# A planner's account of PSUM reads and engine hops, changed for the second stage of a four-layer graph network

## The chip, the cores and the metric

The kernel runs on one core of one Trainium2 chip. The metric is the device time of one launch in microseconds (us), the median of several runs. TensorE is called PE here, VectorE DVE, ScalarE ACT, GpSimd POOL, and SyncE, which issues most transfers, SP. PEld stands for PE's weight loads.

## What is computed

The input x has 128 graphs of 64 nodes with 256 features, 8,192 rows in all, in float32; adj is one 64x64 matrix. Four layers follow one another, each inside a residual sum and a layer norm. The reference, cut to its core:

```python
x = _layernorm(x + _L0(x))   # three products with adj*adj and W1, W2, W3, relu between them
x = _layernorm(x + _L1(x))   # U.T x, W1, relu, W2, U; U = eigenvectors of the normed Laplacian of adj
x = _layernorm(x + _L2(x))   # two graph convolutions, then four LSTMs over windows of the nodes
x = _layernorm(x + _L3(x))   # attention over the 64 nodes of a graph, masked by adj

# in _L2: window length p = 1..4, one LSTM each; the last state of each window replaces its last node
for p in range(1, MAX_SKIP + 1):
    nw = Tv // p
    wins = h[:, :nw * p, :].reshape(Bv * nw, p, Hd)
    last = _lstm_last(Wih[p - 1], Whh[p - 1], bih[p - 1], bhh[p - 1], wins)
    h = h.at[:, jnp.arange(nw) * p + (p - 1), :].set(last.reshape(Bv, nw, Hd))
# one LSTM step
g = x_t @ Wih.T + h @ Whh.T + bias
i, f, gg, o = jnp.split(g, 4, axis=-1)
c = sigmoid(f) * c + sigmoid(i) * tanh(gg)
h = sigmoid(o) * tanh(c)
```

## The kernel before

The rows are cut into 64 tiles of 128 rows, and four tiles make a group, so there are 16 groups. The program has two stages.

**First stage.** It does layer 0 for all groups, and the eigenvectors of one 64x64 matrix beside it, as a long chain of small DVE operations. Its products are recorded at line 926 and those of the eigenvectors at line 286. The change doesn't touch this stage.

**Second stage.** It does layers 1, 2 and 3 group by group. No order of instructions is written in the code. The functions `layer1`, `layer2`, `layer3`, `lstm` and `second` only note operations with the class `Plan`; `Plan.run` then keeps up to four groups (WAYS = 4) under way at once and puts the noted operations into an order. It is a list scheduler: for each engine it looks for the operation that could start earliest by its own account of time, takes the earliest one over all engines, emits it to that engine's queue, and moves the account on. [...] Every instruction emitted so has line 154 in the profile, the line in `emit`.

The account works with three kinds of numbers. A cost is how long an operation holds its engine: for DVE 0.067 + n/960 us for n elements in a partition, for ACT 0.158 + 0.00084 n where it reads PSUM, for PE 0.001673 n + 0.003 us for each product (at least 0.223). LAG (line 110) is the stated hop: how long after that cost another engine may use the result. OWN (line 113) is the same for the engine itself. All are in us.

What waits for what is found in `note` (lines 123 to 147). Each operation lists the parts of tiles that it writes and reads, and a part is a mask over the elements of the tile. An operation waits in the account for every earlier operation on the same tile whose mask and rows overlap with its own, if one of the two writes. This is the account alone. The waits of the built program are set afterwards, by the layer that records instructions: from the order in which operations were emitted, and with more caution than the account, as the profile will show.

**PSUM in the second stage.** There are eight PSUM banks with the tag "ps", each 512 float32 elements in every partition. Most tiles with this tag are filled by a few products and then read as a whole. Two places read a tile in parts:

- `second` (window length 2, second time step) computes the gates of the LSTM from seven products of sums of quarters in place of eight, for each of two halves h. Its helper `two` puts two of these seven products into one bank, in the first and second half of its columns, and hands back both halves; each half is 2 x 128 columns. Each half takes four products, which show as eight matmul records. Then ACT copies p1, and DVE adds p2, p6, p7, p5, p3 and p4 one after the other.
- `layer3` puts the last products of two row tiles into one bank and adds each of them to X by an operation of its own.

The lines of `second` that matter:

```python
p1, p2 = two(0, 1)
S.copy(u1, p1)
V.tensor_add(a, u1, p2)
p6, p7 = two(5, 6)
V.tensor_add(c12, u1, p6)
V.tensor_add(b, c12, p7)
p5, p3 = two(4, 2)
V.tensor_add(d, b, p5)
V.tensor_add(c12, c12, p5)
V.tensor_add(c12, c12, p3)
p4, _ = two(3)
```

In the profile the products with sums of quarters are `ps<-w,sums` and `ps<-hs,sums`, and the DVE additions are `gates<-v,ps` (p2, p6) and `gates<-gates,ps` (p7, p5, p3, p4).

Of the kernel before, what the change touches and what calls it, by code (L numbers as in the profile page):

```python
# [103 lines left out]
class Plan:  # L104
# [2 lines left out]

    LAG = {"PE": 0.205, "DVE": 0.16, "ACT": 0.15, "POOL": 0.0, "SP": 2.0}  # L110

    MOST = {"w": 3, "v": 2, "ps": 4, "gates": 2}
    OWN = {"PE": 0.0, "DVE": 0.125, "ACT": 0.105, "POOL": 0.0, "SP": 0.0}
# [10 lines left out]
    def note(self, engine, calls, cost, ready=0.0):  # L124

        op = Op()
        op.engine, op.calls, op.cost, op.group, op.rank = engine, calls, cost, self.group, len(self.ops)
        op.before, op.after, op.tiles, op.ready, op.start = set(), [], [], ready, None
        for name, args, kw in () if callable(calls) else calls:
            for i, x in enumerate(list(args) + list(kw.values())):  # L130
                if not isinstance(x, Part):
                    continue
                t, write = x.tile, i == 0
                mask = np.zeros(int(np.prod(t.shape[1:])), bool)
                mask[x.at.reshape(-1)] = True
                for other, w, rows, m in t.past:
                    if (w or write) and other is not op and other.start is None and rows[0] < x.rows[1] and x.rows[0] < rows[1] and (m & mask).any():
                        op.before.add(other)
                t.past.append((op, write, x.rows, mask))
                if t not in op.tiles:  # L140
                    op.tiles.append(t)
                    t.left += 1
        op.left = len(op.before)
        for other in op.before:
            other.after.append(op)
        self.ops.append(op)
# [9 lines left out]
    def run(self, groups, ways):  # L156
# [9 lines left out]
        while todo or going:  # L166
# [40 lines left out]
            self.free[e] = t + op.cost  # L207
            end = t + op.cost + self.LAG[e]
            for tile in op.tiles:
# [1329 lines left out]
```

## Time and profile before

| what | value |
|---|---|
| median of three runs | 2520.61 us (2520.24 to 2522.3) |
| the profiled execution's own time | 2522.03 us |
| its span, first to last instruction | 2520.3 us |
| first product of the second stage | at 860.6 us |
| start of the last product | at 2506.2 us |
| PE busy, over the span | 2473.2 us (98%) |
| granted clock of PE | 0.998 |
| HBM traffic | 25.40 MB read, 12.58 MB written |

The span is what the profile's times count from. The profiled execution took 1.7 us more than its span, and it was 1.4 us slower than the median of the runs. Its second stage is some 1,646 us long, with a tail of 14 us of norms and stores after the last product.

A row of the trace's timeline gives the start in us, the duration in us, the engine, the line, the operation, what it writes and reads, and how many were merged into the row; brackets hold the idle time of the engine ahead of it and what ended it. A product of two float32 tiles shows as two matmul records, and matmuls overlap in the record: a matmul with 128 columns is 0.275 us long, and the next one starts 0.112 us after it.

### The profile page before, as it was taken

What the parts mean: (1) busy time and instruction counts of PE and PEld (TensorE: products, weight loads), DVE (VectorE), ACT (ScalarE), POOL (GpSimd) and SP (SyncE); (2) the same over time, 40 slices, a digit from 0 to 9 for tenths busy, and PEclk for the clock granted to TensorE, in tenths of its full rate; (3) what the DMA queues carried; (4) which work ended last, traced back from release to release, by engine and by line L of the source; (5) the groups of instructions that cost most, each with busy time, mean ns of one, the idle gap of its engine ahead of it and who ended that gap; (6) DMA issues with size and microseconds to landing.
All of it is one profiled execution on the core that took longest, in us unless ns stands there. A gap on an engine that the chain in (4) does not pass through costs nothing.

```text
span 2520.3 us, 41153 instructions
## 1 busy us (share of the span) xinstructions
PE 2473.2 (98%) x15788; PEld 2194.3 (87%) x15788; DVE 1523.3 (60%) x5404; ACT 1105.1 (44%) x2754; POOL 139.4 (6%) x317
## 2 busy tenths in 40 slices
PE   9999999999999999999999999999999999999997
PEld 7788888888887889989989899898898998988996
DVE  6888777778885454464554644645546455365336
ACT  2344333333333455444444454444544444445455
POOL 0000000000000100000000000000000001010002
PEclk9999999999999999999999999999999999999999
DMA  4000000000000300000000000000000000000000
GB/s 154 18 10 26 18 17 18 17 18 1 1 1 1 117 1 1 18 18 1 18 18 1 18 1 18 18 1 18 5 5 9 1 9 9 1 9 1 1 1 26
DMA packets 27397, 40.62 MB, mean 16 GB/s; under 512 B 2880, under 2 KB 22080, under 8 KB 27200
## 3 DMA queue, kind: packets, MB, share of 16 engines
q1 hardware_dynamic: 26848, 37.71, 4.4%
q8 instruction: 124, 2.03, 0.3%
q14 instruction: 73, 0.60, 0.1%
q10 hardware_dynamic: 352, 0.28, 0.0%
HBM read 25.40 MB, written 12.58 MB: 15 GB/s over the span
## 4 chain that ended last, share of the span: by engine, by line
PE 91%; DVE 6%; DMA 1%; ACT 1%; issue 1%; POOL 0%; SPq 0%; ACTq 0%; POOLq 0%; DVEq 0%
PE ps L154 60%; PE ps L926 30%; DVE gates L154 2%; ACT gates L154 1%; DVE D L52 1%; DVE X L154 1%; PE pc L286 1%; DMA aw<-in_a_w_dram 0%; DVE c L154 0%; DVE tw L52 0%; POOL rs L154 0%; DVE st L154 0%; DVE w L154 0%; DMA bw<-in_b_w_dram 0%; DMA X<-in_x_dram 0%
## 5 line engine op out<-in xcount | busy, mean ns | idle before, releaser
L154 PE MATMUL ps<-w,wih 128*128 128x128 f32 (+2 forms) x4864 | 839.1, 309 | 1.0 <-ACT v L154 1.0
L154 PEld LDWEIGHTS ps<-w,wih 128*128 128x128 f32 x4864 | 726.6, 191 | 34.7 <-issue 5.0
L154 ACT ACTIVATE gates<-ps,cbi 128x128 f32<-128x128 f32 (+2 forms) x1120 | 447.6, 403 | 508.1 <-PE ps L154 498.2
L154 PE MATMUL ps<-hs,whh 128*128 128x128 f32 (+1 forms) x2816 | 459.3, 286 | 1.7 <-DVE hs L154 1.7
L154 PEld LDWEIGHTS ps<-hs,whh 128*128 128x128 f32 x2816 | 394.9, 191 | 5.4 <-DVE hs L154 3.4
L154 DVE SCALAR_TENSOR_TENSOR gates<-gates 128x256 f32<-128x256 f32 (+2 forms) x256 | 89.9, 351 | 284.2 <-ACT gates L154 283.8
L926 PE MATMUL ps<-aw,h 128*128 128x256 f32 x1024 | 227.2, 379 | 0.0
L926 PEld LDWEIGHTS ps<-aw,h 128*128 128x128 f32 x1024 | 192.9, 190 | 26.0 <-ACT h L935 0.5
L935 ACT ACTIVATE h<-h 128x512 f32<-128x512 f32 x128 | 80.5, 629 | 198.5 <-DVE h L52 198.4
L154 DVE SCALAR_TENSOR_TENSOR c<-gates,c 128x128 f32<-128x128 f32 (+2 forms) x192 | 62.9, 328 | 154.2 <-ACT gates L154 153.2
L154 PE MATMUL ps<-w,sums 128*128 128x128 f32 x896 | 122.5, 280 | 22.7 <-DVE gates L154 22.7
L154 PEld LDWEIGHTS ps<-w,sums 128*128 128x128 f32 x896 | 108.8, 192 | 31.5 <-DVE gates L154 30.7
L154 ACT ACTIVATE gates<-gates,cbi 128x256 f32<-128x256 f32 x128 | 54.9, 497 | 157.8 <-DVE gates L154 157.6
L926 PE MATMUL ps<-ss,tw 128*128 128x256 f32 x512 | 117.9, 380 | 0.0
L926 PE MATMUL ps<-ss,aw 128*128 128x256 f32 x512 | 117.3, 379 | 0.0
L926 PE MATMUL ps<-m,aw 128*128 128x256 f32 x512 | 117.1, 380 | 0.0
L154 DVE SCALAR_TENSOR_TENSOR hs<-gates 128x128 f32<-128x128 f32 (+2 forms) x192 | 62.9, 328 | 87.7 <-ACT gates L154 87.1
L926 PE MATMUL ps<-aw,m 128*128 128x512 f32 x256 | 114.5, 593 | 0.0
L154 POOL TENSOR_SCALAR rs<-mv 128x2 f32<-128x2 f32 x96 | 25.6, 267 | 1530.3 <-DVE mv L154 1529.1
L154 ACT ACTIVATE gates<-c 128x128 f32<-128x128 f32 (+2 forms) x288 | 97.1, 337 | 25.5 <-DVE c L154 24.1
L926 PEld LDWEIGHTS ps<-ss,aw 128*128 128x128 f32 x512 | 96.6, 190 | 12.8
L926 PEld LDWEIGHTS ps<-ss,tw 128*128 128x128 f32 x512 | 96.3, 190 | 12.9 <-issue 0.2
(305 smaller groups left out, 3562.3 us busy)
## 6 DMA issues: line engine op xcount, KB each, us to landing
out_dram<-X SPq DMA_DIRECT2D x64, 128.0 KB, 1.7
X<-in_x_dram SPq DMA_DIRECT2D x30, 256.0 KB, 4.4
rest<-X SPq DMA_DIRECT2D x8, 512.0 KB, 2.6
wih<-in_c_ih_dram SPq DMA_DIRECT2D x4, 1024.0 KB, 7.2
X<-rest SPq DMA_DIRECT2D x8, 512.0 KB, 3.3
aw<-in_a_w_dram SPq DMA_DIRECT2D x3, 1024.0 KB, 10.0
whh<-in_c_hh_dram SPq DMA_DIRECT2D x3, 1024.0 KB, 9.0
aw<-in_a_w_dram SPq DMA_DIRECT2D x1, 512.0 KB, 5.3
```

The costliest lines, as they stand in the source:

```text
L52: return getattr(self.engine, name)(out, *args, **kw)
L154: getattr(e, name)(*[real(x) for x in args], **{k: real(v) for k, v in kw.items()})
L286: PE.matmul(out, lhsT, rhs, start=True, stop=True)
L926: PE.matmul(out, lhsT, rhs, start=start, stop=stop)
L935: S.activation(dst, src, AF.Relu)
```

## The change

There are two edits, both in `Plan`, and both in the account only. The computation stays as it is: the same operations are noted, with the same engines, tiles and costs.

1. A read of a tile with the tag "ps" gets the mask of the whole tile (`...` sets every element). In the account a reader of half a bank so waits for the products of the other half too, where these were noted ahead of it.
2. The stated hop from DVE to other engines goes from 0.16 to 0.13 us and that from ACT from 0.15 to 0.14 us.

```diff
-    LAG = {"PE": 0.205, "DVE": 0.16, "ACT": 0.15, "POOL": 0.0, "SP": 2.0}
+    LAG = {"PE": 0.205, "DVE": 0.13, "ACT": 0.14, "POOL": 0.0, "SP": 2.0}
...
                 t, write = x.tile, i == 0
                 mask = np.zeros(int(np.prod(t.shape[1:])), bool)
-                mask[x.at.reshape(-1)] = True
+
+                mask[... if t.tag == "ps" and not write else x.at.reshape(-1)] = True
                 for other, w, rows, m in t.past:
```

## Prediction

> **What bounds the kernel now.** I began with the page's busy shares, went on to the table by stage, then to who waits for whom on PE, and last to the timeline at one wait. The busy row says that PE is the bound:
>
> ```profile
> PE 2473.2 (98%) x15788; PEld 2194.3 (87%) x15788; DVE 1523.3 (60%) x5404; ACT 1105.1 (44%) x2754; POOL 139.4 (6%) x317
> ```
>
> The change acts only between the first and the last product of the second stage, so that stretch is cut out. The columns are the stretch, its length, and the busy time of PE, PEld, DVE, ACT and POOL.
>
> ```profile
> 860.60:2506.20 1645.60, 1618.22 (x11729) 1495.28 (x11729) 859.99 (x2522) 787.18 (x1975) 97.98 (x201) 1.00 0.03 11
> ```
>
> PE is idle for 1645.60 - 1618.22 = 27.4 us there, while DVE is busy for 860 us and ACT for 787 us, about half of it. Only PE's idle time and the products themselves make this stage long. The waits of PE in this stretch, with total us, times and longest:
>
> ```profile
> PE ps L154 <- DVE gates L154: 22.7, 41, 0.7
> PE ps L154 <- DVE hs L154: 1.7, 2, 0.9
> PE ps L154 <- ACT att L154: 1.0, 2, 0.6
> PE ps L154 <- ACT v L154: 1.0, 2, 0.5
> PE ps L154 <- ACT X L154: 0.6, 1, 0.6
> ```
>
> The five rows make 27.0 of the 27.4 us, and one of them is 22.7: PE fills a bank and waits for DVE, which writes `gates`. The timeline of PE and of DVE at one of the 41:
>
> ```profile
> 1214.14 1.50 PE L154 MATMUL ps<-w,sums 128*128 128x128 f32 x12
> 1216.16 0.94 PE L154 MATMUL ps<-w,sums 128*128 128x128 f32 x6 [0.51 <-DVE gates L154]
> ```
>
> ```profile
> 1214.42 0.42 DVE L154 TENSOR_TENSOR gates<-v,ps 128x256 f32<-128x256 f32 x1 [0.17 <-PE ps L154]
> 1215.68 0.42 DVE L154 TENSOR_TENSOR gates<-v,ps 128x256 f32<-128x256 f32 x1 [0.85 <-PE ps L154]
> ```
>
> DVE's second addition starts at 1215.68, as soon as PE's twelve records are through, and ends at 1216.10; PE goes on at 1216.16. PE waited for a reader which itself had waited for the product right before. The engines take turns where they should overlap. The order of the built program tells why: in the bank of p6 and p7 (and of p5 and p3) the addition of the first half was emitted before the last products of the second half, and the recording layer then makes the next product into that bank wait for the addition, though it writes other columns. The planner didn't know of that wait, since its masks of the two halves don't overlap.
>
> [...] The gap repeats here (three times in the pair step at 1211 to 1226 us, 1.7 us in sum), but what it waits for is a reader of the same tile, so another bank wouldn't end it. [...]
>
> **The change part by part.** The sum is made against the profiled execution, 2522.0 us (span 2520.3 and 1.7 around it). That is 1.4 us above the median of the runs, 2520.6.
>
> *The mask.* It removes no instruction and adds none: 8,120 matmul instructions stand in both built programs. It moves the reads of half banks behind all products of their bank. Comparing the two built orders, before has 69 matmuls in the second stage that wait for an ACT or DVE reader of the bank they write, all in the pair step, and in 41 of these the reader depends on the matmul just before. After has none of the 69. One such wait costs more than its idle time. PE's records start 0.112 us apart and last 0.275, so the idle time in the record begins 0.163 us after the next product was due. Check at the rows above: twelve records from 1214.14 end their turns at 1215.48, the next came at 1216.16, 0.68 us late, which is 0.51 + 0.163. And the six records after it last 0.94 us where 5 x 0.112 + 0.275 = 0.835 would do: 0.10 us more, as the next weight load could not run ahead. Sum: 22.7 + 41 x (0.163 + 0.101) = 33.5 us, all on PE, which sets the end. As a second count, I summed how far each product into `ps` from `sums` starts later than the median spacing of its shape: 34.3 us. The two waits for ACT's `v` (1.0 us) are the same: the copy of p1 ahead of the bank's other half, and with 2 x 0.264 they add 1.5. I take **35.0 us gained**.
>
> *What is late next.* The additions of the first half start up to four products (8 x 0.112 = 0.9 us) later; the copy of p1 is 8 products later in the first pair step (1.8 us). Queued behind them on DVE are the additions of the same bank, then gates of this and other groups; on ACT the gate activations. Who waits for those is PE, at the first product of window length 3, which reads what the pair step wrote. By the orders and spacings, PE has 3.7 to 4.7 us of other products between the two before, and the trace shows no idle time there; after it has 4.2 to 5.2 us in the first 13 groups. The last addition reads p4, whose place hasn't changed. So this costs nothing while that filler stands; without it the chain of one addition (0.42), two activations (0.50 each), two updates of c (0.43 each), a tanh (0.42) and the two writes (0.29 each), some 3.3 us, would show in each of 16 groups. A bank is also held longer by up to 0.9 us; with eight banks the after order has no product which waits for a reader of one of the two matmuls before it, 8 at three matmuls and 16 at four (8 and 11 before), so I price it at nothing.
>
> *The hops.* They change no instruction either, but the order everywhere: PE's, DVE's and ACT's sequences differ in most places, with 1,928 waits of PE for DVE or ACT against 1,841. Is the new hop too short? A DVE operation of 256 elements costs 0.334 us in the account and takes 0.420 in the trace; a matmul released by DVE starts 0.054 us after its end (median of 45). So 0.14 us is the measured hop, and 0.13 is 0.01 us short, where 0.16 was 0.02 us long. For ACT on a bank: 0.373 against 0.471 and 0.053 after the end (7 cases), 0.15 us, so 0.14 is 0.01 us short. Bounds: at most all 1,928 waits come 0.01 us late, 19 us; on the other side the rest of PE's idle time could go, 27.0 - 22.7 - 1.0 = 3.3 us gained. Most waits have slack, as PE idles in 5 other places only; I take 2.0 us lost, some 200 waits of 0.01.
>
> *POOL and SP.* POOL has the same instructions in the same sequence but for the order of groups; SP the same 64 stores of 128 KB and 8 reloads. They follow PE. The DMA queues are 3% busy in this stage. What can move is DVE standing behind POOL's `rs` (X<-rs cost DVE 5.1 us in 9 waits, and two of PE's rows on `hs` stem from such a wait): up to 2 us either way, taken as nothing.
>
> *The tail* after the last product is 14 us of the same norms; the last three products stand in another sequence, by one product of 0.43 us: up to 1 us either way, taken as nothing.
>
> Sum: -35.0 + 2.0 = -33.0 us, so 2489.0 for an execution like the profiled one, and 2520.6 - 33.0 = **2487.6 us** as a median. The case's own range takes 3.3 us gained and 3 more from POOL and the tail below (2481), and hops of 8 us and 3 more above (2497).
>
> **Rivals.** *Part of the stall moves.* The pair step is a dense chain: 56 products of 0.224 us, 12.5 us of PE, and about 20 DVE additions and updates of 0.42 us. The stalls gave DVE time to catch up, and in the account DVE is cheaper than in the trace (0.334 against 0.385 for each of four in a row at 1217.80). If DVE falls behind, each of 16 pair steps gives back about 0.8 us: 13 us, so 2487.6 + 13 = 2501 us. For it: the 10% error. Against: DVE is half idle, and the filler ahead of window length 3 got longer.
>
> *Nothing comes of it.* The waits on half banks could be replaced one for one by waits for whole banks: 2520 us. The 41 to none at one matmul speaks against it.
>
> *Slower.* Reading late holds the banks, and PE waits at the head of the next tile: 16 groups x 2 halves x 4 banks = 128 banks. From 35.0 / 128 = 0.27 us of PE's wait for each bank on, the gain is gone; if the whole 0.45 us, the mean delay of the first half, came through, it would be 58 us, hence 2487.6 + 58 = 2546 us. For it: PE has been without slack. Against: eight banks, and no short loop in the after order.
>
> **How the numbers follow.** Forecast 0.83 (2481 to 2497), stall in part moved 0.10 (2497 to 2506), nothing 0.03, slower 0.04. The range 2481 to 2499 leaves out most of the second case and the last two, with the edges of the first some 0.2. Faster, within and slower than 0.2% (5 us, about what a measurement of this kernel can tell from no change): 0.93, 0.03, 0.04.
>
> **What would show it.** Right: PE's wait for DVE `gates` falls from 22.7 us to under 3; PE's idle time between first and last product from 27 to under 8 us; its busy time there falls also, by some 7 us, since each pause leaves a longer record; `gates<-v,ps` keeps 0.42 us. Wrong: waits of PE on DVE or ACT of many short pieces (hops too short), or a new row of PE waiting at the first product of a bank or of window length 3.

## The result, and the profile after

| | before | after |
|---|---|---|
| median of four runs each | 2520.43 us (2520.13 to 2522.3) | 2485.93 us (2485.29 to 2486.62) |
| the profiled execution's own time, and its span | 2522.03, 2520.3 us | 2486.62, 2484.8 us |
| first product of the second stage | 860.63 us | 859.80 us |
| from there to the start of the last product | 1645.58 us | 1611.15 us |
| from there to the end of the span | 14.1 us | 13.85 us |

The ratio is 0.9862, with a 95% interval of 0.9845 to 0.9879: 34.5 us less by the medians. The spans of the two profiled executions differ by 35.5 us, and 34.4 of these lie between the first and the last product of the second stage, 0.8 ahead of it and 0.25 behind it.

The page of the changed kernel still has PE as the bound:

```profile
PE 2462.3 (99%) x15788; PEld 2191.0 (88%) x15788; DVE 1519.4 (61%) x5404; ACT 1104.5 (44%) x2754; POOL 135.5 (5%) x317
```

The second stage alone, first to last product, with the columns of the prediction's row for this stage (length, then busy time of PE, PEld, DVE, ACT, POOL):

```profile
859.80:2470.95 1611.15, 1607.95 (x11729) 1492.14 (x11728) 856.74 (x2524) 786.60 (x1975) 94.15 (x201) 1.00 0.03 11
```

PE was idle there for 27.4 us and is now for 1611.15 - 1607.95 = 3.2. Who still makes PE wait, in all of the program's products from `emit`:

```profile
PE ps L155 <- ACT X L155: 1.3, 3, 0.9
...
PE ps L155 <- ACT att L155: 0.5, 1, 0.5
PE ps L155 <- ACT v L155: 0.5, 2, 0.3
PE ps L155 <- ACT w L155: 0.4, 2, 0.3
...
PE ps L155 <- DVE hs L155: 0.2, 1, 0.2
```

The row on DVE's `gates`, 22.7 us in 41 waits, is gone. The sequence of a pair step that broke off after twelve records before, on PE and then on DVE:

```profile
1206.03 3.07 PE L155 MATMUL ps<-w,sums 128*128 128x128 f32 x26
1208.93 0.39 PE L155 MATMUL ps<-hs,sums 128*128 128x128 f32 x2
1209.15 0.39 PE L155 MATMUL ps<-w,sums 128*128 128x128 f32 x2
```

```profile
1208.12 0.74 DVE L155 TENSOR_TENSOR gates<-v,ps 128x256 f32<-128x256 f32 x2
1208.78 0.28 DVE L155 SCALAR_TENSOR_TENSOR w<-gates 128x128 f32<-128x128 f32 x1
1208.98 0.41 DVE L155 TENSOR_TENSOR gates<-gates,ps 128x256 f32<-128x256 f32 x1
```

Twenty-six records run through: 25 x 0.112 + 0.275 = 3.07 us, the spacing without a pause, and the next begins at 1208.93. DVE's additions take what they took (`gates<-v,ps` has a median of 0.414 us against 0.420), but two of them follow one another in 0.74 us while PE goes on.

### The profile page after: what moved, and what is told of

Read it like the earlier page. It is cut to its first block, busy times and chain, and to the rows that moved or that the text cites. A ratio compares the mean times of both kernels' runs of the same rounds, so it can differ in the third digit from the quotient of the medians.

```text
span 2484.8 us, 41173 instructions
## 1 busy us (share of the span) xinstructions
PE 2462.3 (99%) x15788; PEld 2191.0 (88%) x15788; DVE 1519.4 (61%) x5404; ACT 1104.5 (44%) x2754; POOL 135.5 (5%) x317
## 4 chain that ended last, share of the span: by engine, by line
PE 95%; DVE 3%; DMA 0%; issue 0%; POOL 0%; ACT 0%; SPq 0%; ACTq 0%; POOLq 0%; DVEq 0%
PE ps L155 63%; PE ps L927 31%; DVE D L52 1%; PE pc L287 1%; DMA X<-in_x_dram 0%; DVE X L155 0%; DVE tw L52 0%; DVE st L155 0%; POOL rs L155 0%; DVE h L52 0%; DVE w L155 0%; DVE u L52 0%; DVE v L155 0%; DVE w L52 0%; DVE ss L52 0%
## 5 line engine op out<-in xcount | busy, mean ns | idle before, releaser
L155 PE MATMUL ps<-w,sums 128*128 128x128 f32 x896 | 113.0, 275 | 0.0
L927 PEld LDWEIGHTS ps<-m,aw 128*128 128x128 f32 x512 | 95.6, 190 | 12.6 <-issue 0.5
```

Source lines behind the costliest of these rows:

```text
L155: getattr(e, name)(*[real(x) for x in args], **{k: real(v) for k, v in kw.items()})
L927: PE.matmul(out, lhsT, rhs, start=start, stop=stop)
```

## Experiments

The theory: PE's waits for a reader of the bank that it is just filling are the whole effect. The rivals: the shorter hops have a share, by another order of everything; what helps is that reads come late; the gain belongs to one chain and not to the number of waits; the hop, and not the bank, paces PE. Times are medians of four runs unless another number is given; each ratio is against the kernel before on the same chip. The intervals are some 4 us wide to either side, so a smaller difference between two kernels rests on their single runs.

| kernel | median, us | ratio (95%) | PE waits for DVE `gates` |
|---|---|---|---|
| mask_alone | 2486.12 | 0.9865 (0.9849 to 0.9882) | none |
| hops_alone (12 runs) | 2521.88 | 1.0009 (1.0001 to 1.0018) | 25.1 us, 41 |
| mask_pair_step | 2487.62 | 0.9872 (0.9857 to 0.9887) | none |
| two_banks | 2482.26 | 0.9852 (0.9837 to 0.9866) | none |
| mask_first_half | 2507.12 | 0.9949 (0.9934 to 0.9964) | 14.0 us, 28 |
| mask_second_half | 2493.64 | 0.9895 (0.9879 to 0.9912) | 4.3 us, 9 |
| mask_hops_far_too_short | 2505.65 | 0.9942 (0.9928 to 0.9957) | none |
| mask_hops_short_by_004 | 2487.12 | 0.9869 (0.9854 to 0.9883) | none |
| mask_hops_far_too_long | 2492.43 | 0.9890 (0.9875 to 0.9905) | none |
| changed_again | 2486.54 | 0.9865 (0.9850 to 0.9879) | none |
| two_banks_new_hops | 2485.44 | 0.9861 (0.9847 to 0.9876) | none |
| ending_norm_on_dve | 2489.26 | 0.9877 (0.9860 to 0.9893) | none |

### One edit at a time

**mask_alone** is the kernel before with the new mask and the old hops.

> Only the mask is changed, the stated hops stay at 0.16 and 0.15 us. Theory (PE's waits for readers of the bank that it fills are the whole effect): the built order has 0 such waits where before has 69, so PE's idle time in the second stage falls from 27 to about 4 us and the time is within 2 us of the changed kernel, 2484 to 2488. Rival (the shorter hops carry a good part of the gain, by another order of everything): at least 5 us of the 34.5 are missing, 2491 or more.

**hops_alone** is the kernel before with the new hops:

```diff
-    LAG = {"PE": 0.205, "DVE": 0.16, "ACT": 0.15, "POOL": 0.0, "SP": 2.0}
+    LAG = {"PE": 0.205, "DVE": 0.13, "ACT": 0.14, "POOL": 0.0, "SP": 2.0}
```

> Only the stated hops are changed, the mask stays. Theory: the built order still has 70 waits for a reader of the bank being filled, 41 of them on a reader of the product just before, as in the kernel before; so the time stays within 3 us of 2520, and PE still waits some 22 us for DVE's gates. Rival (hops carry part of it): 2515 or less. A hop of 0.13 us that is too short would show as many small waits of PE and up to 19 us more.

Measured: 2486.12 and 2521.88 us. The mask has the whole gain, as far as the runs can tell. The hops alone gain nothing: by the medians the kernel is 2.4 us slower than the one before (2521.44 to 2522.92 in 12 runs, 2519.32 to 2520.29 in 15), and the interval puts it 0.01 to 0.18% above. Its waits of PE in the second stage:

```profile
PE ps L154 <- DVE gates L154: 25.1, 41, 0.9
PE ps L154 <- ACT att L154: 1.0, 2, 0.6
PE ps L154 <- ACT v L154: 1.0, 2, 0.5
PE ps L154 <- ACT X L154: 0.6, 1, 0.6
```

DVE's `gates` cost 25.1 us against 22.7, again in 41 waits, but the 1.7 us of waits for `hs` are gone. The second stages of the two profiled executions are about equally long (1645.86 and 1645.58 us), and that of the kernel before took 1.4 us more than the median of its runs. So the traces don't show where the 2.4 us are. The rival with a share of the gain for the hops falls.

**mask_pair_step** sets the whole bank only for the tiles of `two`, and leaves the attention layer's half-bank reads as they were (old hops).

```diff
-                mask[x.at.reshape(-1)] = True
+                mask[... if t.tag == "ps" and not write and len(t.shape) == 4 else x.at.reshape(-1)] = True
```

> The mask of the whole bank only for the tiles with four axes, which are those of the pair step (window length 2, second time step); hops as before. Theory: all 69 waits sit there, so the gain is whole, 2484 to 2488. Rival (the attention layer's half-bank reads have a share): 2 us or more above mask_alone.

Measured: 2487.62 us, 1.5 above mask_alone, where the runs of the two overlap (2486.06 to 2488.26 and 2484.77 to 2487.36). The gain sits in the pair step. A share of the attention layer of 1.5 us or so is neither shown nor excluded.

### Is it the bank, or the late read?

**two_banks** keeps the old mask and the old hops, so that readers may still be emitted early, and takes the shared bank away:

```diff
-                p = ps4((P, 2, 2, P))
+                p = [ps4((P, 2, P)) for _ in which]
...
-                        run(p[:, at, q, :], [(ways[s][weight[i]][:, q, h, :], moving[i][s]) for s in range(2)])
-                return p[:, 0], p[:, 1]
+                        run(p[at][:, q, :], [(ways[s][weight[i]][:, q, h, :], moving[i][s]) for s in range(2)])
+                return p[0], p[-1]
```

> Mask and hops as before, but the pair step puts each of its seven products into a bank of its own in place of two into one; what is computed stays. Theory (the wait is that of the shared bank): the additions may be emitted early as in the kernel before, no product shares a bank with a reader, and the built order has 0 of the 69 waits; the time falls as with the mask, 2484 to 2490, though the step holds seven banks for each half where it held four. Rival (what helped is that the reads come later, behind all products): with early reads the stall stays, 2510 or more. Rival (banks run out): PE waits for readers of other tiles' banks, 2495 or more.

Measured: 2482.26 us (2482.22 to 2482.34), the fastest of all and 1.7 us under the range that I expected. The addition of p6 waits for p6's own last product, four products (eight records) earlier than in the changed kernel. In the first pair step, PE's row that begins with the eight records of p6 and the eight of p7, and DVE's addition of p6, here and then in the changed kernel:

```profile
910.46 2.17 PE L154 MATMUL ps<-w,sums 128*128 128x128 f32 x18
911.55 0.42 DVE L154 TENSOR_TENSOR gates<-v,ps 128x256 f32<-128x256 f32 x1 [0.40 <-PE ps L154]
```

```profile
909.53 2.17 PE L155 MATMUL ps<-w,sums 128*128 128x128 f32 x18
911.52 0.42 DVE L155 TENSOR_TENSOR gates<-v,ps 128x256 f32<-128x256 f32 x1 [0.96 <-PE ps L155]
```

In two_banks eight records are through when the addition starts (910.46 + 7 x 0.112 + 0.275 = 911.52), in the changed kernel sixteen (909.53 + 15 x 0.112 + 0.275 = 911.49). And yet PE doesn't wait for it in two_banks. Its stage, and its waits of PE:

```profile
860.30:2466.40 1606.10, 1604.32 (x11729) 1490.61 (x11729) 858.99 (x2522) 788.42 (x1975) 96.96 (x201) 1.00 0.03 11
```

```profile
PE ps L154 <- ACT att L154: 1.0, 2, 0.6
PE ps L154 <- ACT X L154: 0.6, 1, 0.6
```

1.8 us of idle time in the whole stage. So early reading did no harm here, where the bank isn't shared, and the seven banks that each half takes didn't run out. The rivals of the late read and of the scarce banks both fall.

### Is the gain in proportion to the waits?

**mask_second_half** and **mask_first_half** apply the mask to one of the two halves of the gates (old hops): a tile of `two` carries a mark, set where h == 1 or h == 0.

```diff
-                mask[x.at.reshape(-1)] = True
+                mask[... if not write and getattr(t, "whole", False) else x.at.reshape(-1)] = True
...
                 p = ps4((P, 2, 2, P))
+                p.tile.whole = h == 1
```

> The mask of the whole bank only for the pair step's tiles of its second half of the gates (h = 1); hops as before. The built order has 9 waits on a reader of the product just before, where before has 41. Theory, at some 0.82 us each (idle time, record overlap and the late weight load): 32 fewer make 26 us, so 2494, give or take 3. Rival (the order as a whole, or one chain): the gain isn't in proportion to the waits removed; all of it (2486) or under half (2504 or more).

> The mask only for the tiles of the first half (h = 0); hops as before. The built order has 29 waits on a reader of the product just before. Theory: 12 fewer at 0.82 us make 10 us, so 2510, give or take 3. Rival (not in proportion): within 3 us of 2520, or 2500 or less.

Measured: 2493.64 and 2507.12 us, with the first row of PE's waits in the one and in the other:

```profile
PE ps L154 <- DVE gates L154: 4.3, 9, 0.5
```

```profile
PE ps L154 <- DVE gates L154: 14.0, 28, 0.5
```

| kernel | PE waits for `gates` | idle | products into `ps` from `sums` start late by, in all | us per wait | median less that of mask_alone |
|---|---|---|---|---|---|
| before | 41 | 22.7 us | 34.3 us | 0.84 | 34 us |
| mask_first_half | 28 | 14.0 us | 21.7 us | 0.77 | 21.0 us |
| mask_second_half | 9 | 4.3 us | 7.5 us | 0.83 | 7.5 us |
| mask_alone | 0 | 0 | none | | 0 |

The fourth column is the prediction's second count: how much later than the median spacing of its shape each such product starts. Time goes with the waits, at 0.75 to 0.84 us each, and with the lateness almost to the us. mask_first_half was 2.9 us faster than the estimate, which took 12 fewer waits at a mean price; 13 went, and those of 0.7 us were among them: none over 0.5 is left.

### How much does the stated hop matter?

**mask_hops_far_too_short**, **mask_hops_short_by_004** and **mask_hops_far_too_long** are the changed kernel with other hops:

```diff
-    LAG = {"PE": 0.205, "DVE": 0.13, "ACT": 0.14, "POOL": 0.0, "SP": 2.0}
+    LAG = {"PE": 0.205, "DVE": 0.03, "ACT": 0.04, "POOL": 0.0, "SP": 2.0}
```

(0.10 and 0.11 in the second, 0.40 and 0.40 in the third.)

> The mask as in the changed kernel, and the stated hops cut by 0.10 us more, to 0.03 (DVE) and 0.04 (ACT). Theory (most of PE's 1,900 waits for DVE and ACT have slack, since the planner has other groups' products at hand): some tens of waits come 0.11 us late, 2 to 8 us in all, 2488 to 2494. Rival (the stated hop paces PE, a wait at zero slack is the rule): 500 waits or more at 0.11 us, 55 us, 2540.

> The mask as in the changed kernel, hops of 0.10 (DVE) and 0.11 us (ACT): 0.04 us under the hops measured in the trace of before. With hops short by 0.11 us the time was 19.7 us above the changed kernel. Theory (a loss for each wait without slack, in proportion to what is missing: some 180 waits): 7 us, 2493, give or take 2. Rival (slack takes up small errors, and the loss begins later): under 3 us, 2486 to 2489.

> The mask as in the changed kernel, and both stated hops at 0.40 us. Theory: the planner fills the stated hop with other products where it has them, so 2484 to 2490; only the end, where few groups are left, may lose some us. Rival (a longer hop leaves PE without work, as the emitted order is stretched): 2495 or more.

Measured, with the changed kernel at 2485.93 and 2486.54 us: 2505.65, 2487.12 and 2492.43. The first is 19 us slower, far more than I expected and far less than the rival. Its stage:

```profile
860.30:2490.40 1630.10, 1621.81 (x11729) 1489.81 (x11728) 865.35 (x2526) 790.32 (x1975) 95.24 (x202) 1.00 0.03 11
```

Only 8.3 us are idle time, and PE's busy time is up by 1621.81 - 1607.95 = 13.9 us for the same products: a wait below 0.275 - 0.112 = 0.163 us shows as a longer record and not as a gap. The lateness of the products, summed in the same way, grew by 19.0 us, in pieces all over the stage. At 0.04 us short of the measured hop the loss is 0.6 to 1.2 us by the medians, with runs that overlap, where proportion to the 19 us would have given 7. So the theory of a loss in proportion falls; that slack takes up small errors is the rival that fits. Hops of 0.40 us cost 6 us, between the theory and the rival, and not at the end as I expected, but mostly in one place, where PE ran out of products (and then had a granted clock of 0.50 for 3.41 us, as the last section shows):

```profile
1505.49 0.66 PE L155 MATMUL ps<-ident,att 128*128 128x128 f32 x4 [1.92 <-ACT att L155]
1524.59 2.05 PE L155 MATMUL ps<-adT,X 128*128 128x128 f32 x8 [2.98 <-DVE X L155]
```

### The last 3 us

two_banks is 3.7 us under the changed kernel, but those are two sets of runs, in which the kernel before differs by 0.9 us; beside mask_alone, in one set, it is 3.9 us faster. **changed_again** repeats the changed kernel beside three others, **two_banks_new_hops** has two_banks with the new hops, and **ending_norm_on_dve** changes one line of `layer2` in the changed kernel:

```diff
-            norm(xs[:, t:t + 2, :], g in ENDING)
+            norm(xs[:, t:t + 2, :], False)
```

> The changed kernel once more, beside the three that follow. All theories: 2485 to 2487. If the half-speed stretch of PE at 2442 us, which its first profile shows after 1.3 us of waits for ACT's X, belongs to this order, it is there again.

> A bank of its own for each of the seven products, and the new hops; the mask as before. With the old hops this was 2482.3, 3.6 us under the changed kernel. Theory (the 3.6 us are in the order of the ending, where PE waits for ACT's X and then runs at half speed for 3.4 us): the built order here has the changed kernel's ending, in which a transpose of X stands 15 matmuls behind an addition that it needs, so 2484.5 to 2487. Rival (a bank for each product is better in itself): 2481 to 2483.5.

> The changed kernel, with the norm between layers 2 and 3 of the last two groups applied by DVE and not by ACT; what is computed stays. Theory (PE's waits for ACT's X near 2440 us and the half-speed stretch after them cost some 3 us): without them 2482 to 2484. Rival (DVE, which is busy all through these us, is as late as ACT, or later): 2486 or more.

Measured: 2486.54, 2485.44 (2483.73 to 2487.47) and 2489.26 us. With the new hops two_banks keeps 1.1 us of its lead by the medians, and the runs overlap, so most of the lead seems to belong to an order and not to the banks. But its profiled execution took 2483.73 us, and its granted clock is 1.00 from 2436 to 2450 us, without the half-speed stretch (the last section tells of it), so that stretch can't be what all three orders have in common, and the theory stands only in part. Whether its slower runs had one isn't known, as one execution alone is kept. The norm on DVE failed: the waits for ACT's X went, and another came in their place, longer than all of them:

```profile
PE ps L155 <- ACT att L155: 7.6, 2, 6.6
PE ps L155 <- ACT v L155: 2.5, 3, 1.7
```

```profile
2474.52 0.69 PE L155 MATMUL ps<-ident,att 128*128 128x128 f32 x2 [6.60 <-ACT att L155]
```

The traces divide the difference between two_banks and the changed kernel. The second stage is 1611.15 - 1606.10 = 5.1 us longer in the latter. By the distances between starts of products, 2.5 us of this fall between 2435 and 2450 us: some 1.7 are the half-speed stretch (a granted clock of 0.50 for 3.41 us), the rest the longer waits ahead of it. The other 2.5 us are small pieces ahead of 2435 us, and their cause stays open.

## Why the prediction was right

Forecast 2487.6 us, measured 2485.93; forecast a gain of 33.0 us, measured 34.5. By its own steps:

- **PE bounds the stage, and 22.7 of its 27.4 us of idle time are one wait.** That wait went, and 3.2 us of idle time are left. The forecast was under 8.
- **The mask, -35.0 us.** mask_alone gives 2519.5 - 2486.12 = 33.4 us on its own chip, mask_pair_step 31.9, with the same cause. The price of a wait, idle time and 0.163 + 0.101 us, was right: 0.82 us by the sum, 0.77 to 0.84 in the three kernels of the table on the waits. The mask, which moves the reads behind all products of their bank, and two_banks, in which none of these products shares a bank, both took the 41 waits away. The prediction held that another bank wouldn't end them; with a bank for each product they ended.
- **Nothing is late next.** Right in the main: nothing waits at the first product of window length 3, and the rival of a DVE that falls behind (13 us) didn't come. PE has 0.2 us of waits for DVE left in the stage.
- **Busy time falls.** The forecast said 7 us, and it fell by 1618.2 - 1607.95 = 10.2. The forecast left out the second part of the price, the late weight load, which the record counts as busy: 41 x (0.163 + 0.101) = 10.8. At the prediction's rows the load at 1214.04 us is 0.10 us ahead of its product at 1214.14, and the load behind the wait starts with its product at 1216.16.
- **The hops, +2.0 us: mis-sized.** With the mask at hand, the new hops changed nothing that can be told (2485.93 and 2486.54 against 2486.12). Without it they cost 2.4 us alone, and some 2 us on top of two_banks by the ratios (0.9861 against 0.9852, with intervals that overlap), so their cost seems to depend on the order that comes of it. The step multiplied some 200 waits by 0.01 us, and no run shows such a sum; hops short by 0.04 us cost 0.6 to 1.2 us in all. The upper bound of the same step, 19 us for 0.01, was not near.
- **The sum.** The mask was taken some 2 us too large and the hops 2 us too costly, in opposite directions. That the forecast gain came within 1.5 us of the measured one is in part luck.
- **POOL, SP and the tail, nothing.** The tail moved by 0.25 us and the start of the stage by 0.8. What the forecast didn't see is the ending: three waits for ACT's X, 1.3 us where there was 0.6, and behind them a stretch at a granted clock of 0.50, 3.41 us long, which cost some 1.7 us.
- **The rivals.** "Nothing comes of it" and "slower" are out; a bank that is held longer costs PE nothing that the trace shows (3.2 us of idle time are left in the stage).

## What to carry to other kernels

A planner that orders instructions must know the same hazards as the layer that sets the waits. Where it takes two halves of a bank for separate things and the recording layer doesn't, it emits the reader between two products, for which PE paid 0.77 to 0.84 us each time here; telling the planner, or giving each product a bank of its own, removed it equally. Look for it as short waits of the bound engine (0.5 to 0.7 us) on a reader which itself had waited for the instruction just before, and count the overlap of the records into its price: here the idle column showed two thirds of the loss.

## What the runs showed of the hardware that was not expected

PE's granted clock fell to half for 3.41 us near the end of the changed kernel: in the second stage it is 1.00 up to 2441.63 us, 0.50 from there to 2445.04, and 1.00 again to beyond the last product. The columns are the stretch, its length, busy times, then PE's granted clock:

```profile
2436.00:2440.00 4.00, 3.06 (x26) 2.58 (x24) 4.00 (x18) 2.60 (x7) 3.23 (x10) 1.00 0.01 4
2440.00:2442.00 2.00, 1.34 (x7) 0.87 (x8) 0.49 (x3) 2.00 (x6) 1.68 (x5) 0.91 0.00 0
2442.00:2444.00 2.00, 2.00 (x9) 1.87 (x8) 1.25 (x2) 1.96 (x6) 0.67 (x3) 0.50 0.00 0
2444.00:2446.00 2.00, 2.00 (x9) 1.62 (x8) 1.79 (x9) 0.85 (x2) 0.49 (x2) 0.74 0.00 0
```

The timeline of PE in these microseconds:

```profile
2438.86 0.44 PE L155 MATMUL ps<-ident,X 128*128 128x128 f32 x2 [0.24 <-ACT X L155]
2440.15 0.44 PE L155 MATMUL ps<-ident,X 128*128 128x128 f32 x2 [0.85 <-ACT X L155]
2440.84 0.44 PE L155 MATMUL ps<-ident,X 128*128 128x128 f32 x2 [0.25 <-ACT X L155]
...
2441.65 1.75 PE L155 MATMUL ps<-ident,w 128*128 128x128 f32 x7 [0.26 <-ACT w L155]
2443.20 2.81 PE L155 MATMUL ps<-w,dw 128*128 128x256 f32 x8
```

Eight records of 256 columns take 2.81 us where 7 x 0.216 + 0.38 = 1.89 would do. Four waits of 1.6 us in all, within 3 us, stand ahead of it. It isn't an accident of one execution: the traces of changed_again, mask_alone and mask_pair_step have such a stretch after waits of the same sum, with a granted clock of 0.50 from 2444 to 2446 us. In mask_hops_far_too_long products slow down at two places elsewhere, each at one of its long waits. These rows are the 3.41 us ahead of the first, and the stretch itself:

```profile
1503.54:1506.95 3.41, 0.81 (x6) 0.55 (x6) 1.82 (x5) 1.60 (x4) 0.00 (x0) 1.00 0.00 0
1506.95:1510.36 3.41, 3.41 (x9) 2.70 (x10) 1.52 (x5) 0.09 (x1) 0.00 (x0) 0.50 0.01 2
```

At the second, behind the wait of 2.98 us for DVE's X, eight records of 128 columns from 1524.59 us take 2.05 us, where 7 x 0.112 + 0.275 = 1.06 would do.

The sum of the waits doesn't tell where the clock falls. Between 2436 and 2444 us PE was idle for 1.60 us in the changed kernel, in changed_again and in mask_pair_step, and for 1.59 in mask_alone. In two_banks_new_hops it was idle for 1.60 us there too, with the same 1.3 us of waits for ACT's X, and the granted clock stayed at 1.00. In the kernel before and in two_banks PE waited 0.59 us at this point, at 1.00 as well. So an idle time from which on the clock falls can't be read off these runs.

In the stretch, products of 256 columns start 0.427 us apart in place of 0.216, and those of 128 columns 0.213 in place of 0.112. It cost some 1.7 us, half its length: 2.81 - 1.89 = 0.92 in the eight records of 256 columns, and 1.75 - (6 x 0.112 + 0.275) = 0.80 in the seven of 128 ahead of them. That the waits brought the half clock about is argued from these times; it was not tried on its own and isn't shown.
